# Message sums of a graph layer: order of the partial products, size of the groups, and the engine that weighs the far entries

## The chip, the cores and the metric

The kernel runs on one core of one Trainium2 chip. The core has five engines with one instruction queue each: TensorE (PE in the profile; PEld is its weight load), VectorE (DVE), ScalarE (ACT), GpSimd (POOL) and SyncE (SP), which here only issues DMA transfers. They meet through semaphores. The metric is device time in microseconds, the median of several executions. A profile is one further execution, recorded by the hardware.

## The reference

Four graph layers follow each other on a state `x` of 2708 rows and 128 columns, with one adjacency matrix `adj` of 2708 x 2708, about 2.35% of it non-zero. Only the first layer matters here:

```python
s = node_feats @ msg_w[:, :D].T
d = node_feats @ msg_w[:, D:].T
messages = gelu(s[:, None, :] + d[None, :, :] + msg_b)      # exact gelu
aggregated = einsum('ijd,ij->id', messages, adj)
new_feats = concatenate([node_feats, aggregated]) @ upd_w.T + upd_b
x = layernorm(x + layernorm(gelu(new_feats) + node_feats) * ln_w + ln_b)
```

A message is needed only for a non-zero entry (i, j): `adj[i, j] * gelu(s[i] + d[j] + b)`, summed over j for each row i.

## The kernel before

The first layer goes over the rows in LT = 22 tiles of LR = 125 rows. A row tile is cut into NC = 5 groups of RG = 25 rows, and the 2708 columns j into NB = 22 blocks of JB = 124. In one block every row has CAP = 5 slots. A slot of a row takes its 1st to 5th non-zero column in the block, so that 5 x 25 = 125 of PE's output partitions hold (slot, row) pairs of a group, and the five groups lie side by side in two PSUM banks (`sl`). Entries beyond the fifth in a block are "far"; each row has room for OV = 16 of them over all blocks.

The main loop has 22 x 22 = 484 blocks. A block does the following.

- `pick` (L945 to L955): ten matmuls on PE (L950) with the selection matrix `S` as weights bring, for each group, `d` and the adjacency values of the chosen columns into `sl`, in two FP16 parts (`dA`, 128 + 25 columns). Two more (L955) add `s` of the rows, three groups and two groups at a time, with the weights `same`, 50 partitions high.
- ACT applies GELU to the five groups (and an unused sixth) of `sl` and writes `g` (L1028).
- `weigh` (L1015): DVE multiplies the adjacency columns of `sl` by `own`, which keeps for each partition its own row's value, and writes `W`, the weights of the sum. It is emitted one block late, after the GELU of the next block.
- `add_up` (L958 to L971): for two blocks together, PE multiplies `W` (32 columns wide, FP32) by `g` into `acc`; groups 0 to 3 lie in PSUM quadrants 0 to 3 of column part 0, group 4 in a quadrant of column part 1. After the last pair of a row tile ACT copies `acc` out as `agg`.

`sl` has three buffers and `W` and `g` five. LAG = 3 makes the loop call `add_up` at even blocks, for the blocks four and three back.

The order of work is written out by hand: `Rows.when` gives each step of a row tile a block number at which it is emitted; steps of equal number go by row tile, then by their order in `when`. All queues are in program order. Beside the blocks, these steps run for the coming row tile: `load` and `load_row` (SP: transposed and plain pieces of `adj`), `find` (DVE, L812: the non-zero mask), `rank` (PE L820, then an ACT cast L821: running counts down the columns), `part0` and `part1` (ACT L828, DVE L833: the two FP16 parts of the adjacency values), `slot` (DVE L840: `S` from the ranks), `rank_row`, `past` and `largest_of` (PE L861; DVE L872, L874, L879: the far entries of four blocks, and the eight largest of every two blocks). PE's L820, L861 and the turn share one PSUM bank, `ps`.

For the finished row tile: `largest` (DVE, L885: the 16 largest candidates), `where` (DVE, L910: their columns, two searches, at blocks 1 and 3), `fetch` (POOL, L914: 16 indirect transfers of rows of `d`, added onto `s` that `start_far` put there), `far_gelu` (ACT, L920), `far_sum` (DVE, L926 and L928: one multiply-add for each far entry), `turn` and `close` (PE L934 to L937, ACT L940). The far work of a row tile falls in the blocks of the next: with its own first block as 0, the far GELUs are emitted at blocks 15 and 6 (of the tile after), the eight far sums of each over the four blocks from 17 and from 8.

After the loop comes the tail (`Update`): the aggregate goes through the update weights, and the layer norm follows. The other three layers are not touched.

Of the kernel before, what the change touches and what calls it, by code (L numbers as in the profile page):

```python
# [14 lines left out]
F32 = mybir.dt.float32  # L15
# [157 lines left out]
def gnn_stack(ctx: ExitStack, tc: tile.TileContext, t, out: bass.AP):  # L173
# [378 lines left out]
    with ExitStack() as l0:  # L552
# [10 lines left out]
        with ExitStack() as msg:  # L563
# [6 lines left out]

            DA = D + RG
            dA = [mp.tile([JB, NB, NC, DA], FP16, name=f"dA{q}") for q in range(2)]

# [18 lines left out]
            nc.vector.memset(spread, 0.0)  # L592
            fold = mp.tile([HALF, 32], F32, name="fold")
            nc.vector.tensor_add(fold, ident[:HALF, :32], ident[:HALF, 32:HALF])
            nc.vector.tensor_copy(spread[:, :, :RG], ident[:, :LR].rearrange("p (c i) -> p c i", c=NC))
# [17 lines left out]
            S_all = [mp.tile([JB, HB, NC, P], FP16, name=f"S{n}") for n in range(3)]  # L613
            W_all = [mp.tile([P, 6, 32], F32, name=f"W{n}") for n in range(5)]
            for v in S_all:
# [11 lines left out]
            up = msg.enter_context(tc.tile_pool(name="sums", bufs=2))  # L627
            ep = msg.enter_context(tc.tile_pool(name="slots", bufs=5))
            p_misc = msg.enter_context(tc.tile_pool(name="ps_misc", bufs=1, space=PSUM))
# [6 lines left out]
            def columns_of(sl, a, b):  # L636

                return sl[:, :, :3 * DA].rearrange("p k (c e) -> p k c e", c=3)[:, :, :, a:b]

# [13 lines left out]
            class Piece:  # L653
# [7 lines left out]
                def products(self):  # L661
                    b0, b1, a0, a1 = self.b0, self.b1, self.a0, self.a1
                    psd, pss = (sl_all[(2 * self.n + k) % 3][:, 0, :].rearrange("p (b d) -> p b d", d=D)
                                for k in range(2))
                    d = self.d = ep.tile([P, 6, D], F32, name="g")[:JB, :b1 - b0, :]
                    room = gp.tile([P, 8, D], F32, name="far")
# [36 lines left out]
                def update(self):  # L703
                    ps = p_out.tile([P, PB, D], F32, name="acc")
                    u = ep.tile([P, 6, D], F32, name="g")[:, :self.a1 - self.a0, :]
                    if N < self.a1 * P:
                        nc.vector.memset(u, 0.0)
                    for a, b, r in groups():
                        if self.a0 <= a < self.a1:
                            for i in range(a, b):  # L710
                                nc.tensor.matmul(ps[:r, i - self.a0, :], xT[:, i * P:i * P + r], upd_x,
                                                 start=True, stop=True)
                            nc.vector.tensor_tensor(u[:r, a - self.a0:b - self.a0, :],
                                                    ps[:r, a - self.a0:b - self.a0, :],
                                                    over_tiles(upd_b, b - a, r), op=ALU.add)
                    nc.sync.dma_start(out=u_tab[self.a0 * P:self.a1 * P, :].rearrange("(n p) d -> p n d", p=P), in_=u)
# [21 lines left out]
            class Rows:  # L738
# [9 lines left out]
                def when(self):  # L748
# [25 lines left out]
                    for n in range(OV // 8):  # L774
                        yield b - 1 + n * 9, lambda n=n: self.start_far(n)
                        yield b + 2 + n * 9, lambda n=n: self.fetch(n)
                        yield b + 15 + n * 13, lambda n=n: self.far_gelu(n)
                        for k in range(8):
                            yield b + 17 + n * 13 + k // 2, lambda n=n, k=k: self.far_sum(n * 8 + k)
                    yield b + 36, self.turn  # L780
# [3 lines left out]
                def load_s(self):  # L784
                    self.s3 = up.tile([P, 3, D], FP16, name="s3")
                    for q in range(2):
                        src = sq_tab[q, self.r0:self.r0 + LR, :].rearrange("(c i) d -> i c d", c=NC)
                        for k, (a, e) in enumerate(spans(0, NC, 3)):
                            p = k * HALF + q * RG
                            nc.sync.dma_start(out=self.s3[p:p + RG, :e - a, :], in_=src[:, a:e, :])  # L790

# [72 lines left out]
                def past(self, m):  # L864
                    if m == 0:
                        self.o = op_.tile([P, max(NB * JB, NT * D)], F32, name="o")
                        self.o = self.o[:, :NB * JB].rearrange("p (b j) -> p b j", j=JB)
                        self.cand = vp.tile([P, NB // 2, 8], F32, name="cand")
                        self.count = vp.tile([P, NB], F32, name="count")
# [7 lines left out]
                def largest_of(self, m):  # L877
                    for b in range(m * PB, min((m + 1) * PB, NB), 2):
                        nc.vector.max(self.cand[:, b // 2, :], self.o[:, b:b + 2, :].rearrange("p b j -> p (b j)"))  # L879

# [40 lines left out]

                def far_sum(self, k):
                    w, f = self.v[:, k:k + 1], self.far[k // 8][:, k % 8, :]
                    if k == 0:
                        self.extra = up.tile([P, D], F32, name="extra")
                        nc.vector.tensor_scalar(self.extra, f, w, None, op0=ALU.mult)  # L926
                    else:
                        nc.vector.scalar_tensor_tensor(self.extra, f, w, self.extra, op0=ALU.mult, op1=ALU.add)  # L928

                def turn(self):  # L930
# [5 lines left out]
                    nc.tensor.matmul(ps[:, :P], a[:, 0, :], ident, start=False, stop=False)  # L936
                    nc.tensor.matmul(ps[:, P:32 * NC], a[:HALF, 1, :], fold, start=False, stop=True)  # L937

# [3 lines left out]


                def pick(self, b, sl):

                    h, n = divmod(b, HB)
                    group = [sl[:, c // 3, c % 3 * DA:(c % 3 + 1) * DA] for c in range(NC)]
                    for c in range(NC):
                        for q in range(2):
                            nc.tensor.matmul(group[c], self.S[h][:, n, c, :], dA[q][:, b, c, :],  # L950
                                             start=c % 3 == 0 and q == 0, stop=False)
                    for k, (a, e) in enumerate(spans(0, NC, 3)):
                        p = slice(k * HALF, k * HALF + 2 * RG)
                        out = sl[:, k, :(e - a) * DA].rearrange("p (c e) -> p c e", c=e - a)[:, :, :D]
                        nc.tensor.matmul(out, same[p], self.s3[p, :e - a, :], start=False, stop=True)  # L955

                def add_up(self, pair):


                    if pair[0][0] == 0:  # L960
                        self.acc = p_out.tile([P, PB, D], F32, name="acc")[:, :2, :]
                    jobs = [(b, g, W, c, c * 32, 0) for b, g, _, W in pair for c in range(4)]
                    jobs += [(b, g, W, 4, b % 2 * 32, 1) for b, g, _, W in pair]
                    for b, g, W, c, q, k in jobs:
                        ends = b == NB - 1 and q >= HALF or b >= NB - 2 and k == 1
                        nc.tensor.matmul(self.acc[q:q + 32, k, :], W[:, c, :], g[:, c, :],  # L966
                                         start=b == 0 and k == 0, stop=ends)
                    if pair[-1][0] == NB - 1:
                        self.agg = up.tile([P, 2, D], F32, name="agg")
                        for k, m in ((0, P), (1, HALF)):  # L970
                            nc.scalar.activation(self.agg[:m, k, :], self.acc[:m, k, :], AF.Copy,  # L971
                                                 accum_out=tot[:m, self.t, k:k + 1])

            class Update:
# [11 lines left out]
                def open(self):  # L986
                    room = Values.within(ep.tile([P, 6, D], F32, name="g").rearrange("p a d -> p (a d)"))
                    V = Values.within(ep.tile([P, 6, D], F32, name="g").rearrange("p a d -> p (a d)"))
                    self.st = room.part([P, NT, 6])
# [16 lines left out]

            LAG = 3
            U = Update()
            assert NC == 5 and NB % 2 == 0
            R = [Rows(i) for i in range(LT)]  # L1010
            steps = sorted(((g, n, step) for n, (g, step) in enumerate(x for v in [preparation(), *(v.when() for v in R), U.when()] for x in v)),
                           key=lambda x: x[:2])
            with tc.manual_schedule():
                def weigh(b, g, sl, W):
                    nc.vector.tensor_tensor(  # L1015
                        W[:, :, :RG].rearrange("p (k c) i -> p k c i", k=2), columns_of(sl, D, DA),
                        own[:, None, None, :].to_broadcast([P, 2, 3, RG]), op=ALU.mult)


                late = []  # L1020
                for block in range(LT * NB):
                    i, b = divmod(block, NB)
                    while steps and steps[0][0] < block:
                        steps.pop(0)[2]()
                    sl, W = sl_all[block % len(sl_all)], W_all[block % len(W_all)]
                    R[i].pick(b, sl)
                    g = ep.tile([P, 6, D], F32, name="g")
                    nc.scalar.activation(g.rearrange("p (k c) d -> p k c d", k=2), columns_of(sl, 0, D), AF.Gelu,  # L1028
                                         scale=1.0 / D_SCALE)
# [12 lines left out]
                rest = [step for _, _, step in steps]  # L1042
                assert len(rest) == 11
                last_gelu, far_sums, last_turn = rest[0], rest[1:9], rest[9:]
                G = len(groups())
# [900 lines left out]
```

## Time and profile before

| | us |
|---|---|
| median of 3 runs | 1902.93 (1902.68 to 1903.74) |
| the profiled execution | 1905.26 |
| its span, first to last instruction | 1903.5 |
| first layer's loop, about | 48 to 882 |
| one row tile, from 98 to 765 us | 37.04 |

| engine | busy us | share of the span | busy in one row tile (506.22 to 543.26) |
|---|---|---|---|
| PE | 1626.2 | 85% | 35.45 |
| DVE | 1436.1 | 75% | 34.99 |
| ACT | 1052.1 | 55% | 25.39 |
| POOL | 630.8 | 33% | 25.32 |

A busy share says how long an engine had something in flight. It does not say what it waited for, nor whether the wait mattered. The profile therefore also gives the timeline of an engine (start, duration, line, operation, output and input, and in brackets the idle time ahead of an instruction with what ended it), the waits summed by pair, and the chain of work that ended last. A matmul's end is modelled: PE starts the next one before it, so PE's pace is read from starts.

### The profile page before, as it was taken

The page shows a single profiled execution, that of the slowest core. Times are in us where ns is not written, and L with a number is a line of the kernel's source. Part 1 is how long each engine was busy: PE and PEld are TensorE (multiplying, and loading weights), DVE is VectorE, ACT ScalarE, POOL GpSimd, SP SyncE. Part 2 cuts the span into 40 slices and gives each one's busy share as a digit, 9 for nine tenths or more (in the row PEclk, how much of TensorE's full clock was granted, in tenths as well). Part 3 has the DMA queues.
Part 4 walks back from the last instruction along what each step waited for, and adds up shares of the span by engine and source line. Part 5 has one row for each costly group of instructions (what it writes and reads, how often), then busy time and mean ns, then how long its engine had stood idle before and what let it go on. Part 6 is the DMA issues. An engine that isn't in the chain of part 4 may idle for free.

```text
span 1903.5 us, 36624 instructions
## 1 busy us (share of the span) xinstructions
PE 1626.2 (85%) x14033; PEld 955.4 (50%) x14033; DVE 1436.1 (75%) x3607; ACT 1052.1 (55%) x1538; POOL 630.8 (33%) x426
## 2 busy tenths in 40 slices
PE   5899999999999999986599997577888897199995
PEld 5666666666666666655344443322223343044542
DVE  6899999999999999986678885838886783860104
ACT  3667667666766766654444444458886771430003
POOL 5667766776776677565100000000000000000000
PEclk8899999999999999998699998658998798599997
DMA  8666665666666576533134430032334463354431
GB/s 214 153 130 143 133 144 119 148 122 141 143 131 142 122 149 124 117 69 88 63 123 150 152 112 1 1 106 76 142 137 140 141 199 146 137 204 146 146 121 31
DMA packets 234896, 238.30 MB, mean 125 GB/s; under 512 B 28844, under 2 KB 219630, under 8 KB 228122
## 3 DMA queue, kind: packets, MB, share of 16 engines
q1 hardware_dynamic: 183670, 212.18, 36.1%
q0 software_dynamic: 51040, 23.68, 10.7%
q8 instruction: 112, 1.84, 0.4%
q14 instruction: 74, 0.61, 0.1%
HBM read 220.65 MB, written 15.15 MB: 124 GB/s over the span
## 4 chain that ended last, share of the span: by engine, by line
PE 43%; DVE 28%; POOL 8%; issue 7%; ACT 7%; DMA 5%; DVEq 0%; SPq 0%; ACTq 0%; POOLq 0%
PE acc L1843 10%; POOL far L914 8%; PE lg L1231 5%; PE acc L1238 5%; PE accV L1571 5%; DVE ix L910 5%; PE ps L1499 4%; DMA far<-d_tab,ix 3%; DVE W L1015 3%; PE sl L950 3%; DVE extra L928 2%; DVE o L872 2%; DVE S L840 2%; PE accO L1575 2%; DVE dA L833 1%
## 5 line engine op out<-in xcount | busy, mean ns | idle before, releaser
L914 POOL DMA_INDIRECT far<-d_tab,ix x352 | 563.0, 1600 | 257.5 <-DVE W L1015 110.6
L1028 ACT ACTIVATE g<-sl 128x768 f32<-128x768 f32 x484 | 393.3, 813 | 257.0 <-PE sl L955 201.0
L950 PE MATMUL sl<-dA,S 124*128 124x153 f16 x4840 | 408.2, 231 | 10.1 <-DVE W L1015 7.7
L950 PEld LDWEIGHTS <-S 124*128 124x128 f16 x4840 | 330.4, 98 | 79.7 <-issue 67.9
L966 PE MATMUL acc<-g,W 128*32 128x128 f32 x4840 | 205.5, 277 | 0.5 <-issue 0.5
L966 PEld LDWEIGHTS acc<-g,W 128*32 128x32 f32 x4840 | 140.6, 109 | 58.8 <-issue 55.5
L955 PE MATMUL sl<-s,same 50*128 50x384 f16 x968 | 161.9, 308 | 0.0
L1015 DVE TENSOR_TENSOR W<-sl,own 128x150 f32<-128x150 f32 x484 | 143.4, 300 | 14.6 <-ACT g L1028 13.4
L1232 ACT ACTIVATE w<-lg,row_L_gnn_gate_bias 128x512 f32<-128x512 f32 (+1 forms) x132 | 83.5, 636 | 108.2 <-PE lg L1231 106.9
L1486 POOL TENSOR_TENSOR arena<-arena,off 128x128 f32<-128x128 f32 (+1 forms) x22 | 21.6, 982 | 351.1 <-DMA arena<-in_adjT 321.3
L840 DVE TENSOR_SCALAR S<-rk 124x1000 f16<-124x1000 bf16 (+1 forms) x330 | 133.4, 430 | 0.0
L910 DVE FIND_INDEX8 ix<-v,o 128x8 uint32<-128x2728 f32 x44 | 131.7, 2993 | 0.0
L1571 PE MATMUL accV<-arena,X 128*128 128x512 f32 (+4 forms) x264 | 124.7, 592 | 6.5 <-DVE arena L1537 6.5
L1231 PE MATMUL lg<-qT,mT 128*128 128x512 f32 (+2 forms) x264 | 121.1, 547 | 3.6 <-ACT w L1232 3.1
L1238 PE MATMUL acc<-w,both 128*128 128x512 f32 (+2 forms) x264 | 121.2, 547 | 0.0
L928 DVE SCALAR_TENSOR_TENSOR extra<-far,v,extra 128x128 f32<-128x128 f32 x330 | 114.9, 348 | 6.3
L449 DVE TENSOR_TENSOR g<-ps,row_L_gnn_b 128x512 f32<-128x512 f32 (+2 forms) x14 | 7.9, 574 | 148.1 <-PE ps L447 148.0
L1499 PE MATMUL ps<-XT 128*128 128x512 f32 (+8 forms) x150 | 90.4, 691 | 32.2 <-ACT arena L1505 26.5
L872 DVE SCALAR_TENSOR_TENSOR o<-ps,ar 128x496 f32<-128x496 f32 x132 | 82.4, 624 | 37.0 <-issue 19.7
L1843 PE MATMUL acc<-at,x 128*128 128x512 f32 (+2 forms) x156 | 66.2, 574 | 48.4 <-ACT x L379 48.4
L1233 DVE TENSOR_TENSOR w<-w,at 128x512 f32<-128x512 f32 (+1 forms) x132 | 82.5, 625 | 27.1 <-ACT w L1232 27.1
L879 DVE MAX8 cand<-o 128x8 f32<-128x248 f32 x242 | 90.4, 411 | 0.0
(357 smaller groups left out, 2507.2 us busy)
## 6 DMA issues: line engine op xcount, KB each, us to landing
at<-in_adjT SPq DMA_DIRECT2D x42, 1354.0 KB
ar<-in_adj SPq DMA_DIRECT2D x105, 248.0 KB
far<-s_tab SPq DMA_DIRECT2D x44, 512.0 KB
at<-in_adjT SPq DMA_DIRECT2D x42, 448.0 KB
arena<-in_adjT SPq DMA_DIRECT2D x21, 704.0 KB
arena<-in_adjT SPq DMA_DIRECT2D x21, 650.0 KB
held<-in_adjT SPq DMA_DIRECT2D x7, 1354.0 KB
f_tab<-arena SPq DMA_DIRECT2D x10, 704.0 KB
```

Source lines behind the costliest of these rows:

```text
L840: nc.vector.tensor_scalar(self.S[h][:, :n, :, k * RG:(k + 1) * RG], self.rk[h][:, :n, :LR].rearrange("p b (c i) -> p b c i", c=NC), EDGE + ...
L910: nc.vector.max_index(ix, self.v[:, n * 8:n * 8 + 8], self.o.rearrange("p b j -> p (b j)"))
L914: nc.gpsimd.indirect_dma_start(out=self.far[n][:, k, :], out_offset=None, in_=d_tab[:, :], in_offset=bass.IndirectOffsetOnAxis(ap=self.ix[ ...
L950: nc.tensor.matmul(group[c], self.S[h][:, n, c, :], dA[q][:, b, c, :], start=c % 3 == 0 and q == 0, stop=False)
L966: nc.tensor.matmul(self.acc[q:q + 32, k, :], W[:, c, :], g[:, c, :], start=b == 0 and k == 0, stop=ends)
L1015: nc.vector.tensor_tensor(W[:, :, :RG].rearrange("p (k c) i -> p k c i", k=2), columns_of(sl, D, DA), own[:, None, None, :].to_broadcast([ ...
L1028: nc.scalar.activation(g.rearrange("p (k c) d -> p k c d", k=2), columns_of(sl, 0, D), AF.Gelu, scale=1.0 / D_SCALE)
L1231: nc.tensor.matmul(lg, mT[:, j * P:j * P + r], qT[:, a:b], start=True, stop=True)
L1238: nc.tensor.matmul(acc[k], mrow[:rows[j], j, :], ws[j][:rows[j], a:b], start=j == 0, stop=j == NT - 1)
L1499: nc.tensor.matmul(ps, XT[:, self.js], XT[:, c], start=True, stop=False)
L1571: nc.tensor.matmul(Pair.acc[0][:, a:b], X[:self.r, self.j, :], self.w_[:, a:b], start=first, stop=last)
L1843: nc.tensor.matmul(acc[k], src[:rows[j], j, :], at[:rows[j], a:b], start=j == order[0], stop=j == order[-1])
```

## The change

The s products of `pick` move ahead of the ten other matmuls, into a new function `begin`, which an even block calls for itself and for the next block, into two `sl` buffers. They now start the accumulation in both banks, so they also cover the 25 adjacency columns: `s3` becomes a pair of fixed zeroed tiles that wide. The five groups lie at an even distance of 172 columns, so that GELU and `weigh` address five groups instead of six. In `add_up`, group 4 of four blocks is held back and added together, one block in each quadrant; `fold` and the copies of `acc` cover 128 partitions for it. LAG is 2, so `add_up` comes at odd blocks, for the blocks three and two back. `W` and `g` have six buffers of five groups instead of five of six.

`largest_of` takes the eight largest of four blocks at once. Far entries are weighed by ACT, one instruction for each entry (`far_weigh`, over four blocks from 16 and from 7), and `far_sum` becomes one DVE reduction over eight entries, at blocks 20 and 11, with one addition for the second.

```diff
+            s3_all = [mp.tile([P, 3, DA], FP16, name=f"s3{n}") for n in range(2)]
+            for v in s3_all:
+                nc.gpsimd.memset(v, 0.0)
...
-                return sl[:, :, :3 * DA].rearrange("p k (c e) -> p k c e", c=3)[:, :, :, a:b]
+                return sl.rearrange("p k n -> p (k n)")[:, :NC * PITCH].rearrange("p (c e) -> p c e", c=NC)[:, :, a:b]
...
                         for k in range(8):
-                            yield b + 17 + n * 13 + k // 2, lambda n=n, k=k: self.far_sum(n * 8 + k)
+                            yield b + 16 + n * 13 + k // 2, lambda n=n, k=k: self.far_weigh(n * 8 + k)
+                        yield b + 20 + n * 13, lambda n=n: self.far_sum(n)
...
                 def largest_of(self, m):
-                    for b in range(m * PB, min((m + 1) * PB, NB), 2):
-                        nc.vector.max(self.cand[:, b // 2, :], self.o[:, b:b + 2, :].rearrange("p b j -> p (b j)"))
+                    o = self.o[:, m * PB:min((m + 1) * PB, NB), :]
+                    nc.vector.max(self.cand[:, m, :], o.rearrange("p b j -> p (b j)"))
...
-                def far_sum(self, k):
-                    w, f = self.v[:, k:k + 1], self.far[k // 8][:, k % 8, :]
-                    if k == 0:
-                        self.extra = up.tile([P, D], F32, name="extra")
-                        nc.vector.tensor_scalar(self.extra, f, w, None, op0=ALU.mult)
-                    else:
-                        nc.vector.scalar_tensor_tensor(self.extra, f, w, self.extra, op0=ALU.mult, op1=ALU.add)
+                def far_weigh(self, k):
+                    f = self.far[k // 8][:, k % 8, :]
+                    nc.scalar.activation(f, f, AF.Copy, scale=self.v[:, k:k + 1])
+
+                def far_sum(self, n):
+                    part = up.tile([P, D], F32, name="extra")
+                    nc.vector.tensor_reduce(part, self.far[n].rearrange("p k d -> p d k"), AX.X, ALU.add)
+                    if n:
+                        nc.vector.tensor_tensor(part, part, self.extra, op=ALU.add)
+                    self.extra = part
...
+                def begin(self, sl):
+
+                    for k, (a, e) in enumerate(spans(0, NC, 3)):
+                        p = slice(k * HALF, k * HALF + 2 * RG)
+                        nc.tensor.matmul(columns_of(sl, 0, DA)[:, a:e, :], same[p], self.s3[p, :e - a, :], start=True, stop=False)
+
                 def pick(self, b, sl):
...
-                            nc.tensor.matmul(group[c], self.S[h][:, n, c, :], dA[q][:, b, c, :],
-                                             start=c % 3 == 0 and q == 0, stop=False)
-                    for k, (a, e) in enumerate(spans(0, NC, 3)):
-                        p = slice(k * HALF, k * HALF + 2 * RG)
-                        out = sl[:, k, :(e - a) * DA].rearrange("p (c e) -> p c e", c=e - a)[:, :, :D]
-                        nc.tensor.matmul(out, same[p], self.s3[p, :e - a, :], start=False, stop=True)
+                            nc.tensor.matmul(columns_of(sl, 0, DA)[:, c, :], self.S[h][:, n, c, :], dA[q][:, b, c, :], start=False,
+                                             stop=q == 1 and c in (2, NC - 1))
...
-                    jobs += [(b, g, W, 4, b % 2 * 32, 1) for b, g, _, W in pair]
+                    self.fifth += [(b, g, W, 4, b % 4 * 32, 1) for b, g, _, W in pair]
+                    if len(self.fifth) == 4 or b1 == NB - 1:
+                        jobs += self.fifth
+                        self.fifth = []
...
-            LAG = 3
+            LAG = 2
...
+                    if b % 2 == 0:
+                        for k in range(2):
+                            R[i].begin(sl_all[(block + k) % len(sl_all)])
                     R[i].pick(b, sl)
-                    g = ep.tile([P, 6, D], F32, name="g")
-                    nc.scalar.activation(g.rearrange("p (k c) d -> p k c d", k=2), columns_of(sl, 0, D), AF.Gelu,
+                    g = ep.tile([P, NC, D], F32, name="g")
+                    nc.scalar.activation(g, columns_of(sl, 0, D), AF.Gelu,
                                          scale=1.0 / D_SCALE)
```

## The prediction

> **What bounds the kernel now.** The page first. The chain that ended last names PE, DVE, POOL and ACT in turn, so no total settles it. I cut the trace by the start of the first search (L910), which comes once per row tile: from 98 us to 765 us it returns every 37.04 us. One such tile, with the columns PE, PEld, DVE, ACT, POOL busy, granted clock, DMA share, GB/s:
>
> ```profile
> 506.22:543.26 37.04, 35.45 (x520) 25.50 (x520) 34.99 (x102) 25.39 (x38) 25.32 (x16) 1.00 0.65 136
> ```
>
> PE and DVE are both nearly full; ACT and POOL have 11 us free. Which is the limit shows in the last tile, where nothing of a next tile is left to prepare and DVE is half empty. PE's timeline there (start, length of the modelled span, line):
>
> ```profile
> 859.11 0.84 PE L950 MATMUL sl<-dA,S 124*128 124x153 f16 x10
> 859.88 0.33 PE L955 MATMUL sl<-s,same 50*128 50x384 f16 x2
> 860.14 0.85 PE L966 MATMUL acc<-g,W 128*32 128x128 f32 x20
> 860.92 0.84 PE L950 MATMUL sl<-dA,S 124*128 124x153 f16 x10
> 861.70 0.33 PE L955 MATMUL sl<-s,same 50*128 50x384 f16 x2
> 861.97 0.84 PE L950 MATMUL sl<-dA,S 124*128 124x153 f16 x10
> ```
>
> A pair of blocks takes 861.97 - 859.11 = 2.86 us with no wait: twice (picks 0.77 + s 0.26) and add_up 0.78. Eleven pairs are 31.5. The tile's other PE work by starts: row ranks 1.2, ranks 1.3, turn 1.0. Sum 35.0 of 37.04; 2.0 are waits, the largest this one on PE, once per tile:
>
> ```profile
> 535.04 0.27 PE L820 MATMUL ps<-mask,tri 124*128 124x256 bf16 x1 [1.07 <-ACT rk L821]
> ```
>
> The DVE timeline shows that DVE is as near. From block 15 (529.99) it works without a gap through the searches of blocks 1 and 3, up to the weights of block 4:
>
> ```profile
> 538.34 0.72 DVE L928 SCALAR_TENSOR_TENSOR extra<-far,v,extra 128x128 f32<-128x128 f32 x2
> ...
> 543.25 2.99 DVE L910 FIND_INDEX8 ix<-v,o 128x8 uint32<-128x2728 f32 x1
> ...
> 546.66 2.99 DVE L910 FIND_INDEX8 ix<-v,o 128x8 uint32<-128x2728 f32 x1
> ...
> 549.57 0.29 DVE L1015 TENSOR_TENSOR W<-sl,own 128x150 f32<-128x150 f32 x1
> ```
>
> The W at 549.57 (block 3) ends at 549.86; PE starts the picks of block 6, which reuse that PSUM pair, at 549.92. So PE sets the pace over blocks 6 to 20, and the DVE chain nearly does over blocks 20 to 5. Last, the stretch that no engine can shorten, in the chain:
>
> ```profile
> 820.05 14.07 DMA ar<-in_adj
> ...
> 836.68 10.73 DMA ar<-in_adj
> ```
>
> The row pieces of the last tile land late, and DVE waits for them.
>
> **What the Trainium skill says.** "TensorE: Matmul & The Clock Gate", section "Back-to-back issue gap": warm, N/2.4 + 2.5 ns. For 153 columns that is 66; the trace has (840 - 231)/9 = 68. Its Part 3, "Packing small matmuls", says that different row groups of the array run at once. The trace agrees: an s pair's span, 0.33, is that of its longer half alone (334 ns). The section on the 16 sub-arrays calls ACT and DVE strict FIFO; the 1.07 us above is that, a cast queued behind a dA copy. "SBUF — State Buffer", section "Door 1: The DMA port swizzle", warns that an access crossing 16-byte lines pays. No row here has such a read on DVE.
>
> **The change part by part, per tile.**
>
> *PE.* At each change of array shape the trace shows 0.10 us beyond streaming: the last pick starts at 0.61, streams 0.07, and s starts at 0.77; s streams 384 columns in 0.16 and the next starts after 0.26. Old pair: five changes (pick-s, s-pick, pick-s, s-add_up, add_up-pick). New: add_up-s, s-pick, pick-add_up, so three: -0.20. The s products widen from 384 to 459 columns, 0.16 to 0.19 twice: +0.06. So four s products cost 0.48 (0.58 if a change lies between the two blocks). add_up: 20 records in 0.78 start six waves of 0.107 (four column groups at once, plus 0.14). The fifth groups of four blocks share a wave pair: five of eleven pairs drop to 0.57, -1.07. Together 11 x (-0.14) - 1.07 = -2.6 (-1.5 with the dear s). PE work falls from 35.0 to 32.4.
>
> *DVE.* Weights on 125 instead of 150 columns: 22 x -0.025 = -0.6. MAX8 over 496: L879 is spaced 0.33 for 248, so 0.33 + 248 x 1.04 ns = 0.59 against 0.66, and the later searches read 48 candidates: together -0.5. Sixteen far sums of 0.33 (5.2) become two reductions of 1024 elements and one add. No such reduction is in the trace; a search reads 2728 in 2993 ns, so 1.12 at 1.10 ns an element, and "VectorE: DVE Perf Modes" lists reductions at 1x. The lower end is that, the upper double (2.2) for the 512-byte stride. I take 1.12, as the one-element rate has a row: 2.5 in all, -2.7. DVE work falls by 3.8, to 31.
>
> *ACT.* "ScalarE: Activation LUTs", "What ACT_TABLE_LOAD costs": 186 + 0.833 N, 93 per pointer, 93 overlapped. L379 with two pointers on 128 columns is 479, as stated; one pointer gives 386, spaced 0.29. Sixteen: +4.7. GELU on 640: 22 x -0.107 = -2.4. ACT rises from 25.4 to 27.7. Total free, but not where it falls.
>
> *Moved waits.* begin() fills the next block's PSUM pair too. At an even block PE now stops for the weights and GELU of two blocks back (three before), with ten picks, and every rank product behind it, queued. LAG 2 lets add_up stop for W of one or two blocks back instead of three or four. Two places follow.
>
> Blocks 15 to 19: on ACT the far GELU (0.96), eight scalings (2.35), a dA copy (0.97) and casts queue between GELUs. Walking them in order, the cast that PE's second L820 waits for ends 1.3 us late (1.07 now). The last scaling ends 2.5 us after PE starts the picks of block 19; only then can DVE reduce.
>
> Blocks 20 to 6: the DVE chain in order: reduction 1.12, past(4) 1.3, W 0.2, past(5) 0.8, mask 0.6, W 0.2, largest 0.7, W 0.25, search 3.05, two W 0.5, search 3.05, W 0.25, dA 0.9, W 0.25: 13.2. Now it is 12.5 from 538.34 to the end of block 4's W. PE stands at rank_row(5) for past(4) 1.1, at add_up(0,1) 0.7, add_up(2,3) 0.9, begin(7) 0.2. PE starts block 6 some 16.1 us after block 19, against 13.9 now, with one add_up (0.78) more behind it.
>
> The way on, block 6 to 19, takes 23.15 now. By the new costs: 19.7 with the 1.3, and 0.75 of short stops where ACT is full (blocks 6 to 11): 20.5. Sum 36.6 against 37.04: **-0.44 per tile**; 2.2 of PE's 2.6 turn into waits.
>
> SP's and POOL's queues keep their order and sizes; POOL needs 16 x 1.86 = 29.8 of 36.6, and the first eight fetches land 1.2 us before their GELU (1.9 now).
>
> *How many tiles.* Block 435 issues the first row piece of the last tile; from there to 847.41 the transfers last 60 us whatever PE does. About 19.5 tiles gain: 8.6. The last tile has eight pairs left after its searches, which gain 0.2 each: 1.5. The tail's eight far sums (3.36 us) become scalings and one reduction, the add with it: -0.2. Total -10.3. The profiled execution took 1905.26 (1903.5 and 1.8 around it), 2.3 above the median: 1895.0 for it, **1892.6** for the median.
>
> **The rivals.**
>
> *A, the forecast*: 1892.6; with 36.2 to 36.9 per tile, 1884 to 1900.
>
> *B, the waits are absorbed*: each stop lets the other engines catch up, so that half of the 2.2 vanishes: 35.5 per tile, -1.5 x 19.5 - 1.7 = -31: 1872. For it: in the old trace DVE lags 1.5 us at block 0, all of it backlog that 2.7 us less DVE work could melt. Against: the reduction waits for ACT, not for backlog.
>
> *C, slower: the strided reduction.* At 2.2 us the chain of blocks 20 to 6 grows by 1.1 in every tile, +0.66 per tile net: 19.5 x 0.66 - 1.7 = +11: 1914. It decides from 1.6 us upwards. Against: nothing in the trace shows a stride costing DVE anything.
>
> *D, no change*: the four s products are serial and the short stops add up; 37.1 per tile: 1902. The DVE savings then are only idle time.
>
> **How the numbers follow.** A 0.45, B 0.2, C 0.2, D 0.15. A measurement of this kernel tells about 0.2% (3.8 us) from nothing. Faster: B and nearly all of A, 0.63; same: most of D and a little of A, 0.15; slower: C and a little of D, 0.22. The range for eight in ten, 1868 to 1911, takes in B and most of C; A alone is 1884 to 1900.
>
> **What would show it.** Searches 36.6 us apart. PE: two s pairs in 0.48, add_up in 0.57 and 0.78 by turns. Waits: PE on W at L966 and at the new s products about 1.8 us per tile, PE on L872/L874 at L861 1.1, PE on the rk cast 1.3. The reduction about 1.1 us, idle before it for ACT. Wrong if DVE shows gaps through blocks 20 to 3 (B), or if the reduction is near 2 us (C), or if PE waits for the far GELU, which I hold to be on time.

## The result, and the profile after

| | before | after |
|---|---|---|
| median, us | 1902.81 (4 runs, 1901.2 to 1903.74) | 11144.55 (4 runs, 11142.88 to 11146.38) |
| ratio | | 5.857, 95% interval 5.847 to 5.868 |
| profiled execution, us | 1905.26 | 11142.88 |

The changed kernel takes almost six times as long. No forecast or rival had a number near that. Busy times of the page of after, and its two costliest groups on DVE and ACT:

```profile
PE 9393.6 (84%) x32852; PEld 3466.5 (31%) x32852; DVE 10235.1 (92%) x15403; ACT 8485.2 (76%) x5284; POOL 2624.2 (24%) x1003
...
L1146 DVE SCALAR_TENSOR_TENSOR g<-g,bc 128x1354 f32<-128x1354 f32 x5416 | 8186.7, 1563 | 11.6 <-issue 11.6
...
L1141 ACT ACTIVATE g<-dT,sT 128x2708 f32<-128x2708 f32 x2708 | 6911.4, 2552 | 1279.3 <-DVE g L1146 1279.3
```

These lines did not run at all before. ACT runs a GELU over all 2708 columns once for each of the 2708 rows, and DVE multiplies each result by a full row of `adj`. That is the dense form of the first layer. Cut by time (columns PE, PEld, DVE, ACT, POOL, granted clock, DMA share, GB/s), the trace of after has four parts:

```profile
0.00:923.00 923.00, 783.36 (x11597) 560.05 (x11598) 800.82 (x1929) 624.81 (x1233) 600.13 (x400) 0.97 0.63 133
923.00:1912.00 989.00, 807.14 (x2437) 360.31 (x2437) 610.76 (x1287) 467.05 (x658) 31.20 (x29) 0.87 0.33 117
1912.00:10240.00 8328.00, 7067.32 (x16556) 2220.76 (x16557) 8266.82 (x11034) 6956.91 (x2795) 1971.05 (x548) 0.50 0.03 12
10240.00:11141.00 901.00, 735.79 (x2264) 325.35 (x2262) 556.72 (x1153) 436.45 (x600) 21.79 (x26) 0.89 0.34 122
```

The kernel first runs once as intended: the first layer to 923 us, the other three to 1912. Then it does the first layer again in the dense form, and the other three after it (the third part takes in the beginning of those; the cut at 10240 is only near). The code for this stood in both kernels, outside the functions of the diff:

```python
# check(): per row, far entries counted from the ranks, less those found by the searches (plus equal neighbours)
nc.vector.tensor_tensor(n[:, 2:3], n[:, 2:3], n[:, 0:1], op=ALU.subtract)
nc.vector.tensor_tensor(bad[:, self.t:self.t + 1], n[:, 2:3], n[:, 1:2], op=ALU.add)
# the end of the kernel
with tc.If(counts[0] > 0), ExitStack() as top:
    load_x()
    all_pairs()
    layers_1_to_3(top)
```

`bad` also counts a row whose sums `tot` are not a number. So the kernel guards its sparse path. If a row's far entries do not all turn up among the candidates, it starts over. In the changed kernel the guard fires on this reference's data.

The first pass can still be read. One row tile of it, from first search to first search, answers to the line of 37.04 us before:

```profile
513.49:551.42 37.93, 33.90 (x529) 23.87 (x520) 33.87 (x83) 27.21 (x55) 25.35 (x16) 1.00 0.64 132
```

A tile takes 0.89 us longer than before, not 0.44 less. Layer 1's first weight load is at 922.9 instead of 911.7. So even with the guard silent, the change would have lost some 11 us. These two findings, the guard and the slower tile, are separate, and the experiments take them in turn.

### The profile page after: what moved, and what is told of

It reads as the page before. It is cut to its first block, busy times and chain, and to the rows that moved or that the text cites. A ratio compares the mean times of both kernels' runs of the same rounds, so it can differ in the third digit from the quotient of the medians.

```text
span 11141.1 us, 96761 instructions
## 1 busy us (share of the span) xinstructions
PE 9393.6 (84%) x32852; PEld 3466.5 (31%) x32852; DVE 10235.1 (92%) x15403; ACT 8485.2 (76%) x5284; POOL 2624.2 (24%) x1003
## 5 line engine op out<-in xcount | busy, mean ns | idle before, releaser
L1146 DVE SCALAR_TENSOR_TENSOR g<-g,bc 128x1354 f32<-128x1354 f32 x5416 | 8186.7, 1563 | 11.6 <-issue 11.6
L1145 PE MATMUL bc<-s,sel 75*128 75x512 bf16 (+1 forms) x16248 | 6977.6, 567 | 1219.9 <-DVE g L1146 1215.6
L1141 ACT ACTIVATE g<-dT,sT 128x2708 f32<-128x2708 f32 x2708 | 6911.4, 2552 | 1279.3 <-DVE g L1146 1279.3
L1145 PEld LDWEIGHTS <-sel 75*128 75x128 bf16 x16248 | 2167.4, 134 | 6029.7 <-issue 5920.3
L1134 POOL CAST s<-a 75x2708 bf16<-75x2708 f32 x109 | 265.6, 2437 | 6451.0 <-PE bc L1145 6140.0
L1136 POOL TENSOR_TENSOR a<-a,s 50x2708 f32<-50x2708 f32 x218 | 1162.8, 5334 | 17.6
L1137 POOL CAST s<-a 50x2708 bf16<-50x2708 f32 x218 | 530.0, 2431 | 14.0
L1046 ACT ACTIVATE g<-sl 128x640 f32<-128x640 f32 x484 | 338.1, 705 | 244.6 <-PE sl L964 233.6
L1146 DVE DVE_READ_ACCUMULATOR g<-g,bc 128x1 f32 x5416 | 449.7, 83 | 0.0
L1589 PE MATMUL accV<-arena,X 128*128 128x512 f32 (+1 forms) x528 | 247.8, 589 | 13.0 <-DVE arena L1555 13.0
```

What stands on the lines that cost most here:

```text
L1046: nc.scalar.activation(g, columns_of(sl, 0, D), AF.Gelu, scale=1.0 / D_SCALE)
L1136: nc.gpsimd.tensor_tensor(a[:n, :], a[:n, :], s[:n, :], op=ALU.subtract)
L1137: nc.gpsimd.tensor_copy(s[:n, :], a[:n, :])
L1141: nc.scalar.activation(g, dT, AF.Gelu, bias=sT[:, i:i + 1])
L1145: nc.tensor.matmul(bc[:, c0 - b0:c1 - b0], one, s[:, c0:c1], start=True, stop=True)
L1146: nc.vector.scalar_tensor_tensor(g[:, b0:b1], g[:, b0:b1], 1.0, bc[:, :b1 - b0], op0=ALU.mult, op1=ALU.mult, accum_out=part[:, i, h:h + 1])
```

## Experiments

### Why the dense form runs

The searches were the first suspect. `max` returns eight values, however many far entries the searched columns hold. Counted from the reference's own inputs, row 608 has 1, 9, 2 and 10 non-zeros in blocks 16 to 19. Five of each block fit the slots, so 0 + 4 + 0 + 5 = 9 are far: one more than a search over four blocks can return. It is the only row and search in this data with more than eight, and over two blocks no row has more than seven. The other suspect was the test for not-a-number, since the change lets ACT sum 64 partitions more into `tot`.

**The kernel before, with searches over four blocks and nothing else.**

```diff
-                    for b in range(m * PB, min((m + 1) * PB, NB), 2):
-                        nc.vector.max(self.cand[:, b // 2, :], self.o[:, b:b + 2, :].rearrange("p b j -> p (b j)"))
+                    o = self.o[:, m * PB:min((m + 1) * PB, NB), :]
+                    nc.vector.max(self.cand[:, m, :], o.rearrange("p b j -> p (b j)"))
```

> The kernel before with one edit: the eight largest far entries are taken over four blocks instead of two. Theory (the search loses an entry): counted from the reference's inputs, row 608 has 4 far entries in block 17 and 5 in block 19, nine in the four blocks 16 to 19, where the search keeps eight; the kernel's own count then differs and the first layer is done again by all_pairs, so 11.1 ms. Rival (the widened sums of the fifth groups trip the other half of the test, the one for not-a-number in tot): this kernel has the old fifth groups, so about 1.90 ms.

It took 11124.2 us in its one execution, with the dense rows on its page:

```profile
L1128 DVE SCALAR_TENSOR_TENSOR g<-g,bc 128x1354 f32<-128x1354 f32 x5416 | 8186.1, 1563 | 11.9 <-issue 11.9
```

This one edit is enough to bring it about.

**The changed kernel with searches over two blocks again** (the same edit reversed).

> The changed kernel with one part undone: the searches go over two blocks again. Theory (the search): no all_pairs; the first pass of the changed kernel reached layer 1 at 935.5 us against 924.3 before, so about 1903 + 11 + 1 (five more searches per tile, 0.1 us each on a full DVE in part) = 1914 to 1917, slower than before by 0.6%. Rival (the fifth groups): still 11.1 ms.

1919.0 us, 1.0074 of before (1.0057 to 1.0091). The rest of the change does not trip the guard. It loses 0.7%, a little more than expected.

**The changed kernel with searches over four blocks, shifted by two.**

```diff
-                    o = self.o[:, m * PB:min((m + 1) * PB, NB), :]
+                    o = self.o[:, max(m * PB - 2, 0):min(m * PB + 2, NB), :]
```

> The changed kernel, still with searches over four blocks, but each search takes the last two of one four and the first two of the next (0-1, 2-5, 6-9, ... 18-21). Blocks 17 and 19 of row 608 then fall into different searches, and no row has more than seven far entries in one. Theory (the search): no all_pairs, 1912 to 1916 us. Rival (any other cause in the changed kernel, or searches of 496 columns as such): 11.1 ms.

1912.8 us, 1.0045 (1.0029 to 1.0062). The searches are as wide as in the change. Only their borders moved, so that blocks 17 and 19 fall apart. The width as such is harmless; what fires the guard is nine entries in one search. The three runs together settle it.

### Why the first pass is slower

From here on, a tile's length is the usual distance of its first search to the next tile's in the steady part. Before it is 37.04 us. In the first three rows of the table some tiles are longer (up to 38.96 us with searches of 2), so that their means are 38.03, 38.09 and 37.81.

| version | tile, us | median, us | ratio to before (95%) |
|---|---|---|---|
| changed, first pass | 37.93 | - | - |
| changed, searches of 2 | 37.85 | 1919.0 | 1.0074 (1.0057 to 1.0091) |
| changed, searches of 4 shifted | 37.76 | 1912.8 | 1.0045 (1.0029 to 1.0062) |
| searches of 2, three additions | 36.93 | 1897.9 | 0.9968 (0.9957 to 0.9980) |
| searches of 2, contiguous reduction | 36.37 | 1886.8 | 0.991 (0.989 to 0.993) |
| searches of 2, far sums on DVE | 36.05 | 1878.8 | 0.9870 (0.9853 to 0.9886) |
| the same, begin for each block | 35.97 | 1881.0 | 0.9880 (0.9863 to 0.9896) |
| far sums on DVE, searches of 4 shifted | 35.00 | 1863.6 | 0.9784 (0.9768 to 0.9800) |
| the same, fifth groups of 2 blocks | 35.54 | 1873.5 | 0.9837 (0.9820 to 0.9853) |
| the same, begin for each block | 35.44 | 1872.7 | 0.9830 (0.9814 to 0.9846) |
| before, searches of 4 shifted | 36.89 | 1901.0 | 0.9986 (0.9979 to 0.9992) |

**Far sums on DVE as before, the rest of the change kept** (searches over two blocks).

```diff
-                            yield b + 16 + n * 13 + k // 2, lambda n=n, k=k: self.far_weigh(n * 8 + k)
-                        yield b + 20 + n * 13, lambda n=n: self.far_sum(n)
+                            yield b + 17 + n * 13 + k // 2, lambda n=n, k=k: self.far_sum(n * 8 + k)
...
+                        nc.vector.scalar_tensor_tensor(self.extra, f, w, self.extra, op0=ALU.mult, op1=ALU.add)
```

> The changed kernel with the searches over two blocks and the far entries summed on DVE as before (16 multiply-adds, none on ACT, no reduction). Theory (the strided reduction, 1.93 us where 1.12 was forecast, and the ACT queue ahead of it are what make the loop slower than before): the PE savings of 2.6 us per tile come through in part, 36.0 to 36.6 per tile, 1881 to 1893 us. Rival (the new waits of the paired s products and LAG 2 eat the savings, whatever sums the far entries): 37.0 to 37.5 per tile, 1902 to 1912 us.

1878.8 us, 2 us better than expected. Undoing one part turns a loss of 0.7% into a gain of 1.3%, even though DVE gets back 16 instructions a tile. What that part costs lies in two groups of the changed kernel (DVE, then ACT; from 100 to 760 us):

```profile
L934 DVE TENSOR_REDUCE extra<-far 128x128 f32<-128x1024 f32 x35 | 67.6, 1930 | 9.3 <-ACT far L930 9.1 <-issue 0.2
...
L930 ACT ACTIVATE far<-far,v 128x128 f32<-128x128 f32 x280 | 96.7, 400 | 0.0
```

The scalings cost what was forecast (400 ns, forecast 386). The reduction takes 1.93 us instead of 1.12, and DVE waits for ACT ahead of it. The next two runs part the reduction from ACT's queue.

**Three contiguous additions instead of the reduction.**

```diff
-                    nc.vector.tensor_reduce(part, self.far[n].rearrange("p k d -> p d k"), AX.X, ALU.add)
+                    f = self.far[n]
+                    nc.vector.tensor_tensor(f[:, :4, :], f[:, :4, :], f[:, 4:, :], op=ALU.add)
+                    nc.vector.tensor_tensor(f[:, :2, :], f[:, :2, :], f[:, 2:4, :], op=ALU.add)
+                    nc.vector.tensor_tensor(part, f[:, 0, :], f[:, 1, :], op=ALU.add)
```

> The changed kernel with searches over two blocks, and the strided reduction replaced by three additions of 512, 256 and 128 contiguous elements (same sums, other order); the scaling stays on ACT. Theory (the stride of the reduction is what costs): the additions take 0.58 + 0.33 + 0.22 = 1.1 us as their spacing by rows of the same widths, 0.8 us less than 1.93, so 0.6 to 0.8 us per tile less than with the reduction (37.85), 1902 to 1907 us. Rival (ACT's longer queue is the loss, not the reduction): 1915 to 1920 us as with the reduction.

1897.9 us, 36.93 per tile: 0.92 less than with the reduction, a little more than expected.

**The reduction over neighbouring elements.**

```diff
-                    nc.vector.tensor_reduce(part, self.far[n].rearrange("p k d -> p d k"), AX.X, ALU.add)
+                    nc.vector.tensor_reduce(part, self.far[n].rearrange("p k d -> p (k d)").rearrange("p (d k) -> p d k", k=8), AX.X, ALU.add)
```

> The same, with the reduction reading eight neighbouring elements instead of eight 512 bytes apart. It sums the wrong elements, so this part of the computation is changed: the far sums are not the reference's. Theory (the stride): one reduction 1.1 us instead of 1.93. Rival (reductions of 8 run at this rate whatever the stride): 1.9 us again. Time as with the three additions, within 3 us, if the theory holds.

```profile
L934 DVE TENSOR_REDUCE extra<-far 128x128 f32<-128x1024 f32 x36 | 43.9, 1220 | 9.6 <-ACT far L930 6.9 <-issue 2.7
```

1.22 us for the same 1024 elements: the stride of 512 bytes costs 0.71 each, 1.42 a tile with two of them. The tile falls from 37.85 to 36.37, by 1.48: all of it reached the end. The time, 1886.8, is 11 us below that of the three additions, not within 3 as expected. They take more than their rows suggested: by the groups of that run 708 + 425 + 293 ns against 1220.

With the cheap reduction the ACT path still loses 0.3 us per tile to the 16 multiply-adds (36.37 against 36.05), although it takes DVE work away. DVE was busy 33.11 us of a tile on the ACT path and 34.94 with the multiply-adds. The waits on PE say where the relief went. In one tile of the changed kernel:

```profile
PE ps L867 <- DVE count L880: 1.6, 1, 1.6
PE acc L981 <- DVE W L1030: 1.2, 3, 0.5
PE ps L826 <- ACT rk L827: 1.0, 1, 1.0
```

The first is PE at block 21, held by `past(4)`, which DVE starts only after the reduction. The last is the rank cast queued on ACT behind the scalings and a dA copy. With the contiguous reduction, over a tile from 497.19 us, the first is 0.9 and the last still 1.0. With far sums on DVE, from 491.88 us, the first is 0.8 and the last is gone. So this wait goes with the scalings on ACT, whatever the stride.

### What the other parts are worth

**begin for each block instead of pairs**, on the version with far sums on DVE and searches of two.

```diff
-                    if b % 2 == 0:
-                        for k in range(2):
-                            R[i].begin(sl_all[(block + k) % len(sl_all)])
+                    R[i].begin(sl)
```

> The version with searches over two blocks and far sums on DVE (1878.8 us), with begin called at every block for that block alone. Theory (the pairs save two changes of array shape of 0.10 us each, which outweighs the wait for the block two back): 0.20 us per pair more on PE, 2.2 per tile, of which about 0.7 was waited for anyway: 37.0 to 38.2 per tile, 1900 to 1922 us. Rival (the early wait costs what the changes save): 1872 to 1885 us.

1881.0 against 1878.8 us: the rival's number. I expected the pairs to pay, and here they gave back in waits what they saved: without them PE is busy 35.06 us of a tile instead of 33.52, and its waits in that tile are 0.7 us instead of 2.3.

**Searches over four blocks, shifted, with far sums on DVE.**

> The version with far sums on DVE (1878.8 us), with searches over four blocks shifted by two. Theory (DVE's chain through the searches still holds PE up for about 2 us per tile): the saving of 0.45 us of DVE per tile comes through at 0.2 to 0.4, 1870 to 1876 us. Rival (PE alone bounds it now): 1878 to 1880 us.

1863.6 us, better than expected, and the fastest version: 2.2% below the kernel before. The searches account for about half of the 1.05 us per tile, by their spacing on DVE's timeline (0.33 for each of eleven against 0.59 for five and 0.33 for one, and 88 candidates down to 48: about 0.5). The rest lies in instructions that nobody edited. From 100 to 750 us, with searches of two first, then with shifted ones:

```profile
L845 DVE TENSOR_SCALAR S<-rk 124x1000 f16<-124x1000 bf16 x180 | 80.8, 478 | 0.0
...
L817 DVE TENSOR_SCALAR mask<-at 124x1024 bf16<-124x1024 f32 x36 | 29.4, 816 | 0.0
```

```profile
L845 DVE TENSOR_SCALAR S<-rk 124x1000 f16<-124x1000 bf16 x182 | 74.4, 438 | 0.0
...
L817 DVE TENSOR_SCALAR mask<-at 124x1024 bf16<-124x1024 f32 x37 | 25.1, 679 | 0.0
```

Ten slots at 40 ns and two masks at 137 ns make 0.67 us per tile; with the searches that is a little more than the tile shows. What goes with the slow ones is visible in the traces: the moment at which the instruction begins while POOL issues a fetch. One mask of each version, with the fetch that was running, searches of two first; the masks begin 0.58 and 1.01 us into the fetch:

```profile
503.01 1.61 POOL L919 DMA_INDIRECT far<-d_tab,ix  x1 [0.30 <-issue]
503.59 0.95 DVE L817 TENSOR_SCALAR mask<-at 124x1024 bf16<-124x1024 f32 x1
```

```profile
516.56 1.77 POOL L919 DMA_INDIRECT far<-d_tab,ix  x1 [0.30 <-issue]
517.57 0.68 DVE L817 TENSOR_SCALAR mask<-at 124x1024 bf16<-124x1024 f32 x1
```

The traces of the kernel before, the changed kernel and the eleven experiments have 461 such masks between 100 and 750 us. The 149 that begin 0.55 to 0.83 us after a fetch began take 0.87 us in the mean, and all end 1.49 to 1.53 us after the fetch began. The other 312 take 0.68 in the mean. With searches of two, 33 of 36 masks fall into that stretch; with shifted searches, 1 of 37. The slots show it less sharply. So part of the 15 us is luck: the shorter searches moved the masks and slots to other moments, which nobody had aimed at. No run moved the fetches alone, so that POOL is the cause is likely and not shown.

**The kernel before with the shifted searches alone.**

> The kernel before with searches over four blocks shifted by two, and nothing else. Theory (DVE's chain through blocks 20 to 3 nearly sets the pace already in the kernel before, but PE's own 35.0 us do over the rest): the 0.5 us of DVE per tile bring 0 to 0.3, 1897 to 1904 us. Rival (the searches alone carry the 15 us that they bring to the version with far sums on DVE): 1886 to 1892 us.

1901.0 us over 20 runs, 0.9986 (0.9979 to 0.9992): 0.15 us per tile. The same edit brings 15 us where PE's work is shorter, and 3 where PE's work is the longer. Part of that difference is again the slots: here they stay as they were (444 ns, 439 before), and there they fell from 478 to 438.

**Fifth groups of two blocks**, on the fastest version.

```diff
-                    self.fifth += [(b, g, W, 4, b % 4 * 32, 1) for b, g, _, W in pair]
-                    if len(self.fifth) == 4 or b1 == NB - 1:
-                        jobs += self.fifth
-                        self.fifth = []
+                    jobs += [(b, g, W, 4, b % 2 * 32, 1) for b, g, _, W in pair]
...
```

The fold and the copies of `acc` go back to 64 partitions with it.

> The fastest version so far (1863.6 us: the changed kernel with far sums on DVE and shifted searches), with the fifth group added for two blocks at a time as before. Theory (PE bounds most of the tile, and each of five pairs saves two waves of 0.107 us): 1.07 us per tile more, less what falls into waits, 0.6 to 1.0: 1876 to 1886 us. Rival (DVE bounds it): 1863 to 1867 us.

1873.5 us, 0.54 per tile more, just below what I expected: half of the 1.07 of PE work saved comes through. Ten slots a tile take 461 ns here against 438, so up to 0.23 of the 0.54 may be theirs.

**begin for each block**, on the fastest version (the diff is that above).

> The fastest version so far (1863.6 us) with begin called at every block for that block alone. Theory (as with searches over two blocks, where 1881.0 against 1878.8 showed that the pair's wait gives back what its fewer changes of shape save): 1862 to 1868 us. Rival (with less DVE work the early wait is short, and PE's 0.2 us per pair show): 1880 to 1900 us.

1872.7 us: the expectation fell, and its rival was too high. PE's timeline, first the pairs of the fastest version, then singly:

```profile
519.79 0.56 PE L953 MATMUL sl<-s,same 50*128 50x459 f16 x4
520.28 1.51 PE L960 MATMUL sl<-dA,S 124*128 124x153 f16 x20
521.63 0.38 PE L825 MATMUL ps<-mask,tri 124*128 124x512 bf16 x1
521.95 0.99 PE L977 MATMUL acc<-g,W 128*32 128x128 f32 x16
```

```profile
521.53 0.37 PE L953 MATMUL sl<-s,same 50*128 50x459 f16 x2
521.83 0.84 PE L960 MATMUL sl<-dA,S 124*128 124x153 f16 x10
522.60 0.37 PE L953 MATMUL sl<-s,same 50*128 50x459 f16 x2
522.90 0.84 PE L960 MATMUL sl<-dA,S 124*128 124x153 f16 x10
523.58 0.38 PE L825 MATMUL ps<-mask,tri 124*128 124x512 bf16 x1
523.89 0.85 PE L977 MATMUL acc<-g,W 128*32 128x128 f32 x20
```

From the s products to add_up: 2.16 us in pairs, 2.36 singly. The pair saves 0.20, as forecast, 2.2 us a tile. Of these 0.44 come through, since PE's waits in a tile are 1.6 us with the pairs and 0.3 without. So the pairs went with 9 us here and with 2 on the version with searches of two. How much of that difference is PE's and how much DVE's stays open: without the pairs the slots take 456 ns against 438 here, and 462 against 478 there.

## Why the prediction was wrong

**The step that failed is the one on the searches.** In "The change part by part", DVE, it costed MAX8 over 496 columns by its duration alone: 0.59 against 0.66 us. The price was right (the searches of the changed kernel follow each other by 0.595 us). But it took the search for the same work in fewer instructions, and it is not: eight results now have to cover four blocks. The dense form that follows cost 9232 us (11144.6 against 1912.8 us with shifted searches), a term that the sum had at nothing. None of the rivals had the searches return too little, and neither text named `all_pairs`. The question could have been answered from the reference. By count, 2.38% of the entries are non-zero (not 2.35%), so take 0.0238 as the probability of one. With 124 columns, five slots and independent entries, the chance of more than eight far entries in four blocks is 8.9e-5. Over 2708 rows with five such searches each, 1.2 cases are to be expected; over two blocks 0.37. This one chance outweighed all else in the text.

**The second failure, hidden by the first, is the strided reduction.** The working took 1.12 us, from a search's rate per element, and gave 2.2 as the other end. It measured 1.93, above the 1.6 from which rival C decides. C's number for this, 1914 us, is close to what the shifted searches gave (1912.8) with the guard silent, just above the range for eight in ten. That closeness is partly luck, as two terms of C were off against each other. It had the reduction too dear, at 2.2. And it counted the extra time of only one of the two reductions in a tile, the one in the blocks 20 to 6 (-0.44 + 1.1 = 0.66); measured, both came through, 1.48 for 1.42.

The text also says that the trace before has no such reduction. It has none of this shape, but the later layers have long ones over neighbouring elements:

```profile
L1731 DVE TENSOR_REDUCE both<-room 128x11 f32<-128x1408 f32 x4 | 6.3, 1615 | 1.0 <-ACT room L1727 1.0
```

That is 1.15 ns per element, or 1.17 us for 1024 as an estimate from this line, and it would have confirmed the lower end for neighbours alone (1.22 measured). The line "nothing in the trace shows a stride costing DVE anything" was no evidence: no long reduction of that trace reads at such a stride. The Trainium skill's warning on accesses that cross 16-byte lines ("SBUF — State Buffer", "Door 1: The DMA port swizzle"), quoted in the text and then set aside, pointed the right way; on its size no run says more than these two durations, 1.93 and 1.22 us.

**What held.** Two pairs of lines from PE's timeline of the changed kernel:

```profile
510.93 0.56 PE L957 MATMUL sl<-s,same 50*128 50x459 f16 x4
511.42 1.51 PE L964 MATMUL sl<-dA,S 124*128 124x153 f16 x20
...
529.39 0.64 PE L981 MATMUL acc<-g,W 128*32 128x128 f32 x16
529.97 0.56 PE L957 MATMUL sl<-s,same 50*128 50x459 f16 x4
```

Four s products cost 0.49 us from start to start (forecast 0.48), and an add_up without a fifth group 0.58 (0.57). The stops stood where the walk had put them: at block 21 for `past(4)` 1.6 (1.1, the longer reduction added), for W at add_up 1.2 (1.6), for the rank cast 1.0 (1.3). With the reduction at 1.22, close to the assumed 1.12, the tile was 36.37 even with searches of two; the forecast was 36.6.

**Rival B** said that a stop lets DVE catch up and put the tile at 35.5. With far sums on DVE and shifted searches it is 35.0, so PE can be fed. What stood in the way was the part that was to relieve DVE, and in some versions the slow slots and masks.

## What to carry to other kernels

When an edit makes one instruction do the work of several, ask first what it returns and what guards it: a bound on the number of results is a property of the data, and a fallback that costs almost five times the kernel has to be priced by its probability. Moving work off a full engine did not pay here, because it went into a queue that another engine waits for and came back as one long instruction at the head of the chain: ask both before moving. An access pattern that no row of the trace has is an unknown whose dear end needs its own weight. And before a difference of some tenths of a microsecond per tile is put down to an edit, compare the durations of the instructions that it did not touch.

## What the runs showed of the hardware that I had not expected

- A DVE reduction of 128 x 1024 FP32 to 128 x 128 takes 1.93 us when the eight summands lie 512 bytes apart and 1.22 when they are neighbours.
- DVE instructions that no edit touched (slots, masks) took 438 and 679 ns in one order of work and 478 and 816 in another. A mask that began 0.55 to 0.83 us into one of POOL's indirect fetches took 0.87 us in the mean and ended 1.49 to 1.53 us after the fetch began; at other moments it took 0.68. Whether the fetch is the cause was not tested.
- With two changes of array shape fewer per pair of blocks, PE went from the s products to add_up in 2.16 us instead of 2.36: 0.10 for each, as the prediction had read from the trace before.
